# A graph layer with windows and gathers: the second lane's sort moved behind 32 unrolled sets, and sums stored by SyncE

## The chip, the cores and the metric

The kernel runs on one core of a Trainium2 chip. A time is the device time of one execution in microseconds (us). Before the change the median of 12 runs is 15380.89 us (15371.66 to 15400.01). The trace was taken from one further execution, which took 15393.0 us, with a span of 15391.4 us from its first to its last instruction.

The engines are named as in the profile: PE does the matrix products, PEld loads their weights, DVE is the vector engine, ACT the scalar engine, POOL is GpSimd, and SP is SyncE, which only issues transfers. A transfer issued by SP, ACT or POOL is moved by the core's 16 DMA engines.

## The reference

There are 100,000 nodes with 64 features, and 3,300,000 edges (1.6 million pairs in both directions and one self-loop per node), sorted by their target `dst`; `src` is random.

```
h = max(layernorm(x), 0)
x_e = concat(h[dst], h[src] - h[dst])          # one row per edge
y_e = x_e @ W.T + b
out = x + segment_sum(y_e, dst) / max(segment_count(dst), 1)
```

As the product is linear, the sums over a node's edges of `h[src]` and their count are enough. Nearly all of the work is therefore a sum of 3.3 million rows of 64 numbers, picked at random out of 100,000. The kernel keeps each row of `h` as three bf16 parts and a one (`h3`, 193 used numbers, 388 bytes), so that sums on PE are exact enough.

## The kernel before, in words

**First stage** (0 to about 450 us): `h`, `h3`, the node's own product `hb`, and zeros in the sum array `acc` (65 numbers per node, in HBM).

The edges are then handled in two ways at once.

**Windows.** The first 256 x 7968 edges are cut into 256 windows of 7968 edges each, whose targets span at most 256 nodes. Four windows make a set, so there are 64 sets in two lanes of 32 sets. For each lane `sort_lane` (L418) sorts 128 windows at once by source, each in a partition of `keys`, in a bitonic network: `exchange` (L454) copies one half of a piece to a buffer `tmp` on ACT (L455) and takes the minimum and maximum on DVE (L456, L457). The buffer is in PSUM, pieces have up to 1536 numbers. `fill_lane` (L621) then fetches the sorted keys column by column with indirect transfers of POOL (`kf` L636, `kx` L721) and stores index lists `sr_d`, `dt_d`, `et_d`, `xs_d` in HBM.

`quads` (L740) handles sets. A set goes through the 157 column tiles of `h3` (640 rows each; `tables` is a copy in HBM, three tiles to one load `tab`, L761, of 727.5 KB). In a step of two tiles DVE makes one-hot matrices `gh` (L789) and `dh` (by the helper at L340), PE picks rows with them (`pick`, `gp` L811, 12 products), ACT copies them to bf16 (`gs` L813), and PE adds them to the windows' nodes (`put`, `total` L819, 32 products). A set has 79 steps. At its end the four sums are copied (`whole` L835, which marks the end of a set in the trace), corrected on DVE, and added to `acc` by four accumulating transfers that POOL issues (L849).

**Gathers.** The other edges are 352 chunks of 28 x 128 edges (`chunks`, L345). POOL fetches 128 rows of `h3` in one indirect transfer (`nb`, L391: 9,856 of them), DVE makes a one-hot matrix `hot` of 14 x 128 columns (L340) and PE sums into `ps` (L396). The chunk's sum is added to `acc` by POOL again (L366 with indices, L371 in the loop).

**The order** is the program's order on each engine, and generators interleave it: whoever emits a piece of sort or of a set also asks for a number of gathers. The sorts of lane 0 and lane 1 follow each other (with lane 0's `fill_lane` beside lane 1's sort), paced at 1250 ns of estimated sort work per gather. Then come four sets written out, and then a hardware loop of three passes (L909) with 20 sets and 98 chunks each, about 1.7 gathers per step. Additions are put off by 56 gathers and kept 8 gathers (`GAP`) apart. At its end each pass drains its gathers and additions.

**Last stage**: a flag `odd` tells whether some assumption on the data failed (then loops repeat everything in a slow way; they run no pass otherwise); the division, the product with `W` and the sum with `x` follow in 28 steps of `acc`, `hb` and `x`.

Of the kernel before, what the change touches and what calls it, by code (L numbers as in the profile page):

```python
# [32 lines left out]
LANES = 2  # L33
SB = 20
KB = 98
U0 = 4
KG = 16
# [3 lines left out]
STEP = 1050  # L41
GAP = 8
# [19 lines left out]
PIECE = 1536  # L62
COUNTS = 1
GAIN = 2.0 ** 40
PART = 1024
TG = 3
SL = 8
SUB = 8
# [16 lines left out]
def plan(v, e):  # L85

    wl = 1 << int(np.log2(33 * CH * 1.05))
    ew = wl - PAD
    nw = LANES * P
    chunks = -(-(e - nw * ew) // CHUNK)  # L90
    return wl, nw, max(chunks, (nw // W - U0) // SB * KB)


@with_exitstack
def gnn_preln(ctx: ExitStack, tc, x, src_w, dst_w, src_p, dst_p, src_a, dst_a, wT, b, out, V, E):
# [27 lines left out]
    SETS = NL * G  # L123
    NCB = -(-V // CS)
    NE = NCB + 1
    NG = -(-NCB // SL)
    AHEAD = 8
# [3 lines left out]
    PA = NCH - (SETS - U0) // SB * KB  # L131
# [4 lines left out]
    assert 2 * C == P and NCB % 2 == 1 and PA >= 0 and SL % 2 == 0  # L136
# [9 lines left out]
    wb_d = dram.tile([SETS * W, 1], I32, name="wb_d")  # L146
    ksort = dram.tile([NL * P * WL + NT * P, 1], I32, name="ksort")
    sr_d = dram.tile([SETS, NCB, 2, P], I16, name="sr_d")
    dt_d = dram.tile([NG, P, SETS, SL * 2 * D], I16, name="dt_d")
# [25 lines left out]
    wb_r = consts.tile([1, SETS * W], I32, name="wb_r")  # L175
    turns = consts.tile([1, 2], I32, name="turns")
    ones = consts.tile([P, 1], F32, name="ones")
# [4 lines left out]
    odd = consts.tile([P, 1 + 5 * LANES], F32, name="odd")  # L182
# [22 lines left out]
    with tc.tile_pool(name="pre", bufs=2) as pre, tc.tile_pool(name="small", bufs=4) as small, \  # L205
# [32 lines left out]
        most = small.tile([P, NMT], F32, name="most", bufs=1)  # L238
        nc.vector.memset(least, 0.0)
        nc.vector.memset(most, 0.0)  # L240

        def bounds(m):
# [3 lines left out]
            nc.vector.tensor_reduce(least[:n, m:m + 1], d[:n], axis=AX.X, op=ALU.min)  # L246
            if m == NMT - 1:

                nc.vector.scalar_tensor_tensor(d[:n], d[:n], float(V), d[:n], op0=ALU.is_lt, op1=ALU.mult)
            nc.vector.tensor_reduce(most[:n, m:m + 1], d[:n], axis=AX.X, op=ALU.max)  # L250
            if m < NMT - 1:
                return
            span = small.tile([P, NMT], F32, name="span", bufs=1)
            nc.vector.tensor_sub(span, most, least)
            nc.vector.tensor_reduce(odd[:, 0:1], span, axis=AX.X, op=ALU.max)
            nc.vector.tensor_scalar(odd[:, 0:1], odd[:, 0:1], float(P), None, op0=ALU.is_ge)
# [55 lines left out]
    with tc.tile_pool(name="rows", bufs=6) as rows, \  # L312
# [5 lines left out]
        def number(at, engine, most):  # L318
            with tc.issue_after(last[engine].ins):
                return nc.values_load(at, engines=[engine], min_val=0, max_val=most)  # L320
# [4 lines left out]

        later = []
        count = [0, 0]
# [4 lines left out]
        def add_now(all_of_them=False):  # L332
            while later and (all_of_them or (later[0][0] <= count[0] and count[0] - count[1] >= GAP)):
                later.pop(0)[1]()
                count[1] = count[0]

# [8 lines left out]
        def chunks(first, n, dynamic=None):  # L345


            def load(q):
# [3 lines left out]
                nc.sync.dma_start(si[:, :k], src_p[at].rearrange("k p j -> p k j"))  # L352
                di = index.tile([P, KG, J], I32, name="di")
                nc.sync.dma_start(di[:, :k], dst_p[at].rearrange("k p j -> p k j"))
                rel = index.tile([P, KG, J], F32, name="rel", bufs=1)
                nc.vector.tensor_sub(rel[:, :k], di[:, :k], base_b[:, at][:, :, None].to_broadcast([P, k, J]))
                near = index.tile([P, KG, J, D], I16, name="near")
                nc.vector.tensor_scalar(near[:, :k], rel[:, :k, :, None].to_broadcast([P, k, J, D]), float(2 * CH), None,
                                        op0=ALU.min)
                to = index.tile([P, KG], I32, name="to", bufs=3)  # L360
                nc.vector.tensor_scalar(to[:, :k], base_b[:, at], pcol, None, op0=ALU.add)
                return si, near, to

            def addition(q, rows_to, sums):
                if dynamic is None:
                    nc.gpsimd.indirect_dma_start(  # L366
                        out=acc, out_offset=bass.IndirectOffsetOnAxis(ap=rows_to, axis=0),
                        in_=sums, in_offset=None, compute_op=ALU.add)
                else:
                    at = number(base_r[0:1, ds(dynamic + q, 1)], POOL, V)  # L370
                    nc.gpsimd.dma_start(acc[ds(at, P)], sums, accum_op=ALU.add)  # L371
# [687 lines left out]
```

## Time and profile before

| what | us |
|---|---|
| median of the runs | 15380.89 |
| profiled execution, whole / span | 15393.0 / 15391.4 |
| first gather issued by POOL | 439 |
| lane 0's sort ends (its `at_i` is made) | 1578 |
| lane 1's sort ends | 2582 |
| set 1, 4, 5 end (first `whole` copy) | 3031, 3556, 3880 |
| the loop's passes, mean distance of ends of sets | 187.3, 187.4, 186.6 |
| distance across the border of two passes | 249, 246 |
| last set ends; last stage's first load issued | 15029; 15075 |

The distances are read from the starts of the first `whole` copy of each set. A set outside the borders takes 187 us, so sixty sets make up three quarters of the time. In a row of a group view, "x2468 | 2356.2, 955 | 752.0" is the number of instructions, their busy time in us, the mean of one in ns, and the idle time of their engine just before them, with what ended it. In a row of a timeline the first two numbers are start and duration in us. "issue" is idle time for which the profile shows no cause outside the engine.

### The profile page before, as it was taken

Reading aid. Unit: us, or ns where it says so; the run is one execution under the profiler, and the core shown is the slowest. Engines: PE = TensorE matmul, PEld = TensorE weight load, DVE = VectorE, ACT = ScalarE, POOL = GpSimd, SP = SyncE. Lnnn points to the kernel's source line nnn. Section 1 sums busy time; section 2 is a strip of 40 time slices with the busy share of each in tenths; the row PEclk is TensorE's granted clock in tenths of the full one; section 3 lists DMA queues with packets and bytes.
Section 4 is the critical chain, followed back from the end, with each engine's and each line's share of the span. In section 5 each row is a group of like instructions: output and inputs, shape, how many; then the busy total and the mean of one; then the engine's idle time right before and its main releaser. Section 6 shows DMA issues by size and latency. Waiting matters only on the chain. (4 is left out here: it accounts for less than half of the span.)

```text
span 15391.4 us, 559362 instructions
## 1 busy us (share of the span) xinstructions
PE 11557.9 (75%) x238778; PEld 9470.2 (62%) x238778; DVE 11308.9 (73%) x15452; ACT 6113.0 (40%) x11710; POOL 11139.4 (72%) x11210
## 2 busy tenths in 40 slices
PE   6101001596999988998799898999879999999985
PEld 5100001475777777777677777777767777777775
DVE  6889797675777777777677777777767777777774
ACT  5335344242444444444344444444434444444441
POOL 4776766546777777777677777777777777777776
PEclk7555555798999999999899999999999999999997
DMA  7683233796999999999899999999989999999997
GB/s 294 124 104 55 48 52 76 184 310 217 317 315 310 312 305 307 307 314 302 263 315 323 306 309 305 310 307 311 304 264 311 320 312 313 307 310 310 311 303 282
DMA packets 1746424, 4097.89 MB, mean 266 GB/s; under 512 B 943899, under 2 KB 952230, under 8 KB 1738950
## 3 DMA queue, kind: packets, MB, share of 16 engines
q1 hardware_dynamic: 1182534, 3461.26, 64.5%
q0 software_dynamic: 454208, 535.92, 17.2%
q10 hardware_dynamic: 107168, 64.74, 2.4%
q8 instruction: 1877, 30.75, 0.8%
q14 instruction: 637, 5.22, 0.1%
HBM read 3880.72 MB, written 219.04 MB: 266 GB/s over the span
## 5 line engine op out<-in xcount | busy, mean ns | idle before, releaser
L391 POOL DMA_INDIRECT nb<-h,si x9856 | 9433.3, 957 | 3285.8 <-issue 2804.8
L813 ACT CAST gs<-gp 128x386 bf16<-128x386 f32 x10048 | 4837.4, 482 | 7098.5 <-PE gp L811 6869.9
L811 PE MATMUL gp<-tab,gh 128*128 128x193 bf16 x60288 | 6235.6, 251 | 942.2 <-DMA tab<-tables 562.2
L811 PEld LDWEIGHTS <-gh 128*128 128x128 bf16 x60288 | 4890.0, 99 | 1964.2 <-issue 927.9
L340 DVE TENSOR_TENSOR dh<-dt,c 128x1024 bf16<-128x1024 int16 x5056 | 3450.2, 682 | 2864.9 <-PE total L819 2719.9
L789 DVE TENSOR_TENSOR gh<-srs,c 128x1536 bf16<-128x1536 int16 x5056 | 4761.0, 942 | 18.4 <-PE gp L811 17.1
L819 PE MATMUL total<-gs,dh 32*128 32x193 bf16 x160768 | 4418.6, 247 | 37.3 <-issue 35.0
L819 PEld LDWEIGHTS <-dh 32*128 32x128 bf16 x160768 | 3198.8, 94 | 1075.7 <-issue 1056.6
L396 PE MATMUL ps<-nb,hot 128*128 128x193 bf16 x9856 | 1807.0, 263 | 2505.5 <-DVE sums L409 1870.5
L396 PEld LDWEIGHTS <-hot 128*128 128x128 bf16 x9856 | 971.3, 103 | 2466.8 <-DVE sums L409 1921.5
L455 ACT COPY tmp<-keys 128x1536 f32<-128x1536 f32 (+14 forms) x540 | 650.4, 1214 | 1238.1 <-DVE keys L457 1016.9
L456 DVE TENSOR_TENSOR keys<-tmp,keys 128x1536 f32<-128x1536 f32 (+14 forms) x540 | 755.2, 1419 | 90.4 <-ACT tmp L455 89.5
L340 DVE TENSOR_TENSOR hot<-near,c 128x1792 bf16<-128x1792 int16 x704 | 759.6, 1079 | 9.3 <-PE ps L396 9.2
L457 DVE TENSOR_TENSOR keys<-tmp,keys 128x1536 f32<-128x1536 f32 (+14 forms) x540 | 755.1, 1417 | 2.3
L849 POOL DMA_DIRECT2D acc<-wsums x256 | 348.3, 1360 | 199.6 <-DVE dh L340 60.8
L636 POOL DMA_INDIRECT kf<-ksort,at_i x322 | 310.7, 965 | 98.7 <-issue 90.4
L371 POOL DMA_DIRECT2D acc<-sums x294 | 301.8, 1027 | 15.1 <-DMA acc<-wsums 7.6
L407 DVE TENSOR_REDUCE sums<-ps 128x64 f32<-128x192 f32 x352 | 123.2, 350 | 157.0 <-PE ps L396 156.8
L839 DVE SCALAR_TENSOR_TENSOR whole<-own,whole 128x193 f32<-128x193 bf16 x512 | 190.9, 413 | 41.8 <-ACT whole L835 41.2
L303 PEld LDWEIGHTS o_ps<-w_own,hT 128*128 128x128 f32 x784 | 156.0, 253 | 81.0 <-ACT hT L298 71.1
L366 POOL DMA_INDIRECT acc<-sums,to x58 | 94.6, 1632 | 149.8 <-DVE sums L409 129.7
L721 POOL DMA_INDIRECT kx<-ksort,xat x128 | 120.8, 944 | 111.2 <-DVE xat L718 57.7
(174 smaller groups left out, 3565.4 us busy)
## 6 DMA issues: line engine op xcount, KB each, us to landing
tab<-tables SPq DMA_DIRECT2D x3328, 727.5 KB
srs<-sr_d SPq DMA_DIRECT2D x1216, 512.0 KB
nb<-h,si POOLq DMA_INDIRECT x9856
tables<-h ACTq DMA_DIRECT2D x157, 242.5 KB
h<-parts SPq DMA_DIRECT2D x28, 1358.0 KB
acc<-zeros SPq DMA_DIRECT2D x28, 910.0 KB
at<-acc SPq DMA_DIRECT2D x28, 910.0 KB
xt<-in_x SPq DMA_DIRECT2D x28, 896.0 KB
```

Of the source, the lines that this page charges most:

```text
L340: nc.vector.tensor_tensor(out.rearrange("p k (a d) -> p k a d", d=D), numbers[:, :, None].to_broadcast(shape), upto[:shape[0], :n].rearran ...
L391: last[POOL] = nc.gpsimd.indirect_dma_start(out=nb[:, j], out_offset=None, in_=h3, in_offset=bass.IndirectOffsetOnAxis(ap=si[:, u, at:at + ...
L396: nc.tensor.matmul(ps, lhsT=before[0][:, j], rhs=before[1][:, j, :CE], start=before[2] == 0 and j == 0, stop=before[2] == parts - 1 and j ...
L455: last[ACT] = nc.scalar.copy(tmp, lo)
L456: nc.vector.tensor_tensor(lo, tmp, hi, ALU.min)
L457: last[DVE] = nc.vector.tensor_tensor(hi, tmp, hi, ALU.max)
L636: last[POOL] = nc.gpsimd.indirect_dma_start(out=kf[:, c], out_offset=None, in_=ksort, in_offset=bass.IndirectOffsetOnAxis(ap=at_i[:, c0 + ...
L789: nc.vector.tensor_tensor(gh[:, :m].rearrange("p c i b s -> p (c i) b s"), srs[u, s // SL][:, c:c + m].rearrange("p c i s -> p (c i) s")[: ...
L811: nc.tensor.matmul(gp[:, i], lhsT=ghots[t][:, i, b], rhs=row[:, b + i * (NB - NR), :CE], start=b == 0, stop=b == NR - 1)
L813: nc.scalar.copy(gs[t], gp)
L819: nc.tensor.matmul(total[:, i, to(b)], lhsT=hot[at, b * P:b * P + P], rhs=of[at], start=flags.get("start", False) and b == 0, stop=flags.g ...
L849: nc.gpsimd.dma_start(acc[ds(at, CH)].rearrange("(b p) c -> p b c", p=P), sums, accum_op=ALU.add)
```

## The change

- Lane 1 is no longer sorted ahead of the sets. Lane 0 is sorted (its pieces of the first pass are 512 wide), 32 calls of its `fill_lane` follow, and then 32 sets start. In the first 69 steps (`late=True`) each step also takes four calls of `fill_lane(0)` and 4800 ns worth of POOL's fetches. From then on each step gives 0.9 units to lane 1's sort and fill (a call costs one unit and its estimated ns / 1500). Its pieces have up to 1024 numbers and its `tmp` lies in SBUF (pool `tmp`, one buffer), as PSUM is taken by the sets. In it the copy of an exchange is two calls ahead of its minimum and maximum, and all counting is left to ACT.
- The second 32 sets are written out too, without a loop. Eleven of the 53 table loads of a set are kept in SBUF for them (`kept`).
- Gathers are spread evenly: about as many per step over all sets (`pace`), chosen anew for the second half.
- `sync`, `fetched_rows` and `numbers_in` chain the instructions of SP and POOL in the order in which the program emits them.
- Sums of sets and chunks are no longer accumulated by POOL. SP stores them plainly (`put`), and reads the one row that the next one shares and writes it to `side_w` or `side_c` (`shared`), 4 gathers later (`GAP = 4`). The first three chunks' sums are kept and added at the end, where five indirect additions also put the side rows back. New flags check that ranges follow each other.
- A gather takes 128 edges in a row, so that its targets lie in a band of 32 nodes, and `hot` is written only there (`BAND`), in buffers zeroed once.
- `dt` is loaded for 32 tiles at once instead of 8, index loads are for 8 chunks instead of 16, and `rows` has 5 buffers instead of 6.

```diff
-LANES = 2
-SB = 20
-KB = 98
-U0 = 4
-KG = 16
+PARTS = (32, 32)
+U1 = 32
+KG = 8
-GAP = 8
+BEHIND = 0.9
+BAND = 32
+GAP = 4
+EARLY = 3
+KEEP = 5
-PIECE = 1536
+PIECE = (1536, 1024)
@@ chunks
-            def addition(q, rows_to, sums):
-                    nc.gpsimd.indirect_dma_start(
-                        out=acc, out_offset=bass.IndirectOffsetOnAxis(ap=rows_to, axis=0),
-                        in_=sums, in_offset=None, compute_op=ALU.add)
...
+                def put():
+                    at = number(base_r[0:1, c], SP, V)
+                    sync(acc[ds(at, P)], sums)
+
+                def shared():
+                    at = number(base_r[0:1, after], SP, V)
+                    sync(side_c[c], acc[ds(at, 1)])
+
+                add_later((LAG - 1) * J, put)
+                add_later((LAG - 1) * J + GAP, shared)
@@ sort_lane
+            def both(part, n):
+                finish = part()
+                if soft:
+                    yield 0
+                    yield 0
+                finish()
+                yield 2.083 * n + 290
@@ quads, the same for the four sums of a set
-                        nc.gpsimd.dma_start(acc[ds(at, CH)].rearrange("(b p) c -> p b c", p=P), sums, accum_op=ALU.add)
+                    sync(acc[ds(at, CH)].rearrange("(b p) c -> p b c", p=P), sums)
...
+                if s < NCB and s % TG == 0 and kept is not None and s // TG % KEEP == 0:
+                    tabs[u, s // TG] = kept[:, s // TG // KEEP]
@@ the order
+                    begin = fill_lane(0, fill, took)
+                    for _ in range(4 * SL):
+                        next(begin)
+                    rest = behind_quads()
+                    left = 0.0
+                    pace = (NCH * J - count[0]) / ((SETS - 1) * NE // 2)
+                    for i, _ in enumerate(quads(0, U1, late=True)):
+                        if i < NE // 2 - 10:
+                            for _ in range(4):
+                                next(begin, None)
+                            gathers(FILL)
+                        else:
+                            drain(begin)
+                            left += BEHIND
+                            with behind_hots():
+                                while left > 0:
+                                    left -= 1 + next(rest, 0) / 1500
+                            gathers(pace * GATHER)
                     drain(rest)
+                    add_now(True)
...
+                pace = (NCH * J - count[0]) / ((SETS - U1) * NE // 2 - 4)
+                for _ in quads(U1, SETS - U1, kept):
+                    gathers(pace * GATHER)
                 drain(ev)
                 add_now(True)
-                with tc.For_i(0, (SETS - U0) // SB, 1) as g:
...
+                for q, sums in enumerate(early):
+                    at = number(base_r[0:1, q:q + 1], POOL, V)
+                    nc.gpsimd.dma_start(acc[ds(at, P)], sums, accum_op=ALU.add)
```

## The prediction

> **What bounds the kernel now.** I read the page's slices first, then stages, then POOL's groups inside the loop, then PE's waits there.
>
> ```profile
> core 0: us, PE busy (x) PEld busy (x) DVE busy (x) ACT busy (x) POOL busy (x), PEclk, DMA share, GB/s
> 500.00:1590.00 1090.00, 115.40 (x756) 101.06 (x756) 993.99 (x955) 427.82 (x466) 774.22 (x777) 0.54 0.56 80
> 1590.00:2590.00 1000.00, 74.73 (x423) 57.14 (x424) 845.36 (x1123) 397.01 (x449) 691.45 (x714) 0.52 0.29 50
> 3217.00:3566.00 349.00, 323.38 (x7112) 264.67 (x7110) 263.42 (x369) 150.02 (x313) 169.31 (x171) 0.98 0.93 308
> ```
>
> The stages: lane 0's sort, lane 1's sort, and two of the written-out sets. The sorts keep DVE busy (994 of 1090 us) and leave PE at a tenth; the sets keep PE busy and DVE at three quarters. In the sets with few gathers POOL is half idle.
>
> ```profile
> L391 POOL DMA_INDIRECT nb<-h,si x2468 | 2356.2, 955 | 752.0 <-issue 701.1 <-DMA nb<-h,si 21.3 <-PE gp L811 18.0
> L849 POOL DMA_DIRECT2D acc<-wsums x72 | 98.2, 1364 | 57.2 <-DVE dh L340 22.7 <-DVE gh L789 15.8 <-DMA acc<-wsums 9.1
> L371 POOL DMA_DIRECT2D acc<-sums x89 | 91.6, 1029 | 0.1
> L778 POOL DMA_INDIRECT rows_x<-h,xs x36 | 34.8, 967 | 11.0 <-issue 11.0
> ```
>
> These are POOL's groups from 4000 to 7400 us, in the loop's first pass. Busy and idle together are 3108 + 155 + 92 + 46 = 3401 us, the whole window, and the idle part is a constant 0.30 us after every gather:
>
> ```profile
> 5013.41 0.94 POOL L391 DMA_INDIRECT nb<-h,si  x1 [0.30 <-issue]
> 5014.66 0.95 POOL L391 DMA_INDIRECT nb<-h,si  x1 [0.30 <-issue]
> ```
>
> One gather per 1.25 us is all that POOL does, so POOL bounds the loop, although the page gives it 72%. A gather costs (2356.2 + 752.0) / 2468 = 1.259 us there. Per set: 137 gathers and 2 of `rows_x` make 175 us, four `acc<-wsums` at 2.16 us 8.6, 4.9 `acc<-sums` at 1.03 us 5: 189 against 187 measured. PE is close behind:
>
> ```profile
> PE gp L811 <- DMA tab<-tables: 142.7, 174, 3.1
> PE ps L396 <- DMA nb<-h,si: 76.6, 73, 4.2
> ```
>
> PE's undisturbed step takes 2.07 us with two gather products in it and 2.00 with one (timeline at 5000 us). So a set is 79 x 1.92 + 0.08 per gather + 6 at its end, 169 us with 137 gathers, and 8 us of waiting for tables (142.7 / 18 sets) make 177. The written-out sets with 80 gathers or so took 171 to 178 us.
>
> **The change part by part.** The sum goes along the time axis of this profile.
>
> *To the end of lane 0's sort.* It ends at 1578 us. The 51 `hot` in it shrink from 1.08 us (1792 numbers) to 0.39 (448 numbers; read from `dh` forms of 1024 in 0.686 and 512 in 0.421), 35 us less on a DVE that is the bound; 512-wide first pieces add 5. First-stage `bounds` gets eight more passes over 3584 numbers, about 30 us of DVE where it has a third of its time free: 0 to 15; I take 0. End: 1548.
>
> *First set.* Lane 0's fill now lies in front. 32 fetches at 1.25 us are 40, and 10 for the store and reload of the lists. Then 69 steps at 4800 ns of fetches, which POOL needs in full: 331 us. Ten ordinary steps 23, and 20 for the end that waits for the last lists. 424 us: set 1 ends at 1972.
>
> *How many gathers remain.* Lane 0's yields sum to 876 us, so 701 gathers are asked for. The first set asks for 265 fetches, 225 of them the fill's (161 `kf`, 64 `kx`), so 40 gathers. 9115 remain. The pace is (9856 - 701) / 4977 = 1.84 fetches per step; the first half's other 2459 steps ask for 4523, including lane 1's 225. That is 145.4 per set. 4817 are left for 32 sets, 150.5 each.
>
> *POOL without sums.* 294 + 256 + 58 accumulations leave POOL (302 + 348 + 95 us busy). Per set in the first half 147.4 fetches x 1.259 = 185.6 us, in the second 152.5 x 1.259 = 192.0.
>
> *Lane 1 behind 31 sets.* Its calls cost 2043 units, 2270 of the 2459 steps at 0.9: it just fits, with no burst at the end. DVE's load per set, from the loop's rows: `gh` 74.9 us, `dh` 54.3, `eh`, `whole` and sums 10.6, narrow `hot` 10.4 x 0.39 = 4, together 144. Lane 1 adds 755 us of minima and maxima (half of the page's two rows), 15 for 69 more pieces, 64 before and 155 after the sort, so 989 / 31 = 32. 176 of 192 us, 92%. ACT: 78 us per set, and 18 more for copies (325 us and more per lane) and counts. PE: 1.92 x 79 + 0.08 x 145 + 6 + 8 = 178. All lie under POOL; I take no stall from them, and keep their failure as a rival.
>
> *Two SBUF inputs.* Before, `tmp` was in PSUM. Now minimum and maximum of lane 1 read two SBUF operands. The trace has DVE instructions of that form beside gathers at the start of the sort:
>
> ```profile
> 475.93 1.28 DVE L447 COPY_PREDICATED s<-own,q 128x1024 int32<-128x1024 int32 x1
> 476.19 1.86 POOL L391 DMA_INDIRECT nb<-h,si  x1 [0.30 <-issue]
> ...
> 477.85 1.22 DVE L443 TENSOR_TENSOR own<-s,keys 128x1024 int32<-128x1024 int32 x1
> 478.36 1.53 POOL L391 DMA_INDIRECT nb<-h,si  x1 [0.30 <-issue]
> ...
> 698.37 1.73 DVE L457 TENSOR_TENSOR keys<-tmp,keys 128x1530 f32<-128x1530 f32 x1
> 699.13 0.94 POOL L391 DMA_INDIRECT nb<-h,si  x1 [0.30 <-issue]
> ```
>
> The gather that starts inside such an instruction takes 1.5 to 1.9 us; the one beside an exchange with `tmp` in PSUM takes 0.94. From 450 to 520 us 48 gathers take 1158 ns each, 10 us more than at 944, beside 20 such instructions: 0.5 us each. A pair of 2.4 us delays one gather, perhaps a second: between 0 and 1.0 us; I take 0.6. 339 pairs make 203 us on the engine that bounds, between 0 and 339.
>
> The Trainium skill (SBUF — State Buffer, Who interferes with whom) says that a DVE instruction with two SBUF inputs contends with a GpSimd instruction that reads SBUF, and that the second to start blocks fully until the first is done. This speaks against the change; if gathers were held for the whole of both instructions, 339 x 2.4 = 820 us would be lost and the sum would be 15,118, while by the rows above it is 203.
>
> *SP.* It gets two transfers for each of 256 + 349 sums, in order with its table loads, and each waits for the landing of the one before. In the loop a 1 KB load of SP (`xs`) lands 4.9 us after its issue in the median, 6.8 at most (DMA records of 58 of them), and the pairs are 4 gathers, 5.0 us, apart: between 0 and 1.8 us of standing, I take 0.3. 18 per set, 5 us, which delay table loads that wait for a free buffer anyway. PE has 14 us per set of cover under POOL. Cost nothing; the cover ends at 0.8 us each.
>
> *Transfers.* `kept` takes a fifth of the table bytes off the second half, `dt` has a quarter of its packets: at best the 8 us of waits per set, hidden under POOL. `KG`, five `rows` buffers: nothing, POOL still leads by 70 gathers. Unrolling: the instruction queues already moved 36 MB for 559,362 instructions, so the loop saved no fetch; its borders (249 and 246 us instead of 187, and the drain before it) go, one switch of pools comes: 25 us.
>
> *Tail.* Before, 362 us from the last set's `whole` to the end. The five last additions (one each 3.75 us) leave POOL, 24 less; six pairs on SP at 6 us follow, 36; three early additions 11, five side additions with their indices 20: 405.
>
> **Sum**: 1548 + 424 + 31 x (185.6 + 6.5) + 25 + 32 x 192.0 + 405 = 14,501 us. The profiled execution (15391.4) stands 0.07% above the median of the runs; on that scale 14,490.
>
> **Rivals.**
> 1. *Gathers are not held up.* The pairs run on DVE where gathers slip between: the 203 us and part of the 25 go, and POOL's bare 1.25 us holds: 14,501 - 203 - 60 = 14,240. For it: the fetch reads only an index column. Against: 1.86 and 1.53 above.
> 2. *DVE's queue becomes the bound of the first half.* DVE at 92% with a pair of 2.4 us where a step leaves 0.44 us free; `gh` has three buffers. At 205 us per set it is 13 x 31 = 400 more: 14,900. For it: the DVE waits for PE's release in the loop (788.6 us in 18 sets) are all its slack, 44 us per set, and lane 1 uses 32. Against: those waits show it ahead of PE.
> 3. *SP starves the tables; slower than before.* Stores and reads stand in SP's queue in front of `tab`. From 178 us PE must reach 192 + 880 / 63 = 206 per set, 1.6 us for each of 18 pairs' halves. Fully exposed at 3.75 us it would be 245, and 17,800. For it: SP stands 1,575 us before `tab` in 18 sets, so it never is ahead by more than three buffers. Against: 5.0 us of spacing.
> 4. *The slow way is taken* because a new flag rises: many times the time. From the reference's inputs the windows' first nodes are at least 235 apart and chunks reach 7 of the band's 16, so this is nearly out.
>
> **How the numbers follow.** My case 0.45 (14,330 to 14,700), rival 1 0.18, rival 2 0.24, rival 3 0.12 (most of it above 15,400), rival 4 0.01. Faster by over 0.2%, about what a measurement can tell, is all but rivals 3 and 4, and small milder forms: 0.87; within 0.2% 0.01; slower 0.12. The range takes in rival 1 without its full 60 us and rival 2 with a little more: 14,170 to 15,000, leaving out rivals 3 and 4 and some 0.07 at the ends.
>
> **What would show it.** POOL's four rows should become two, with a gather to gather distance of 1.25 us in both halves and more than 0.95 us of duration beside lane 1's pairs. Sets should end 192 us apart in both halves. `ACT tmp` and `DVE keys` should run up to about the 30th set. PE's wait for `tab` should stay near 8 us per set. Wrong would be: PE waiting for `gh` by tens of us per set (rival 2), or for `tab` with SP standing before `acc<-wsums` (rival 3).

## The result, and the profile after

The changed kernel takes 15,144.9 us in the median of 7 runs (15,128.9 to 15,197.1) beside 15,383.3 us for the kernel before, a ratio of 0.9847 with a 95% interval of 0.9838 to 0.9856. It is faster, as forecast, but by 238 us and not by 890, and it lies above the predicted range. The profiled execution has a span of 15,152.9 us.

The stages of the changed kernel, in the same columns as before: the sets 2 to 24, which have lane 1's sort beside them; the sets 25 to 30, which have lane 1's fill beside them; and the sets of the second half.

```profile
core 0: us, PE busy (x) PEld busy (x) DVE busy (x) ACT busy (x) POOL busy (x), PEclk, DMA share, GB/s
1989.90:6793.00 4803.10, 4045.81 (x84367) 3317.01 (x84366) 3772.88 (x5369) 2147.79 (x4240) 3374.44 (x3401) 0.94 0.87 281
6793.00:8250.00 1457.00, 1076.37 (x21844) 879.59 (x21842) 898.72 (x1579) 540.26 (x1114) 859.75 (x906) 0.87 0.91 251
8650.00:14780.00 6130.00, 5516.01 (x117912) 4539.55 (x117909) 4222.15 (x6430) 2466.97 (x5153) 4596.02 (x4864) 0.96 0.84 264
```

The second half is what was forecast: 6130 us for 32 sets, 191.6 each with the switch of pools. PE is busy 90% of it. In the sets 2 to 24 PE is busy 84% and DVE 79%, in the fill PE 74%: there neither is full, and the time must be in waits. The distances between the `whole` copies give the account, against the sum of the prediction (14,501 in the time of the profile):

| Step | Predicted, us | Measured, us | Difference |
|---|---|---|---|
| end of lane 0's sort | 1548 | 1460 | -88 |
| first set | 424 | 529 | +105 |
| sets 2 to 24, each | 192.1 | 209.3 | +396 in all |
| sets 25 to 30, each | 192.1 | 242.7 | +304 in all |
| sets 31 and 32, together | 384 | 390 | +6 |
| switch and second half | 6169 | 6131 | -38 |
| tail | 405 | 373 | -32 |

The differences sum to 653 us; the spans differ by 652. So the miss lies in the first half. POOL's groups there, from 2500 to 6400 us (mean duration of one; idle time before, and what ended it):

```profile
L353 POOL DMA_INDIRECT nb<-h,si x2729 | 2717.0, 996 | 833.7 <-issue 800.1 <-DMA nb<-h,si 15.5 <-PE gp L917 14.0
L353 POOL DMA_INDIRECT rows_x<-h,xs x36 | 34.4, 956 | 315.1 <-DMA xs<-xs_d 294.9 <-issue 20.2
```

A gather costs (2717.0 + 833.7) / 2729 = 1.301 us. The prediction had 1.259 and 6.5 us a set for the held ones (gathers that last longer beside lane 1's DVE instructions), 1.303 in all. That price was right, and yet POOL is not the bound: for 295 us it stands in front of `rows_x`, waiting for the last lists of a set, 16 us in each of the 18.6 sets of the window. POOL is ahead of the quads and waits for them. PE's waits in the same window (who waited for whom: total us, number, longest us):

```profile
PE ps L450 <- DVE sums L464: 263.5, 89, 8.3
PE gp L917 <- DVE gh L891: 218.7, 165, 7.4
PE gp L917 <- DMA tab<-tables: 98.3, 108, 5.0
```

The two longest of DVE's waits in the same window, in the same columns:

```profile
DVE gh L891 <- DMA srs<-sr_d: 563.9, 207, 8.3
DVE gh L891 <- PE gp L917: 201.0, 153, 5.5
```

The waits of SP's queue there, three of which are for transfers that it issued itself:

```profile
SPq L349 <- PE gp L917: 2136.8, 805, 10.8
SPq L349 <- DMA side_w<-acc: 136.3, 48, 5.7
...
SPq L349 <- DMA acc<-wsums: 61.2, 32, 4.5
SPq L349 <- DMA acc<-sums: 54.0, 31, 4.0
```

PE waits 580 us, 31 us a set; 8 were forecast, all for tables. Most of it is for DVE: for its sums of the gathered rows (there is one PSUM buffer `ps`) and for its one-hots `gh`. But DVE isn't full. It stands 564 us, 30 us a set, before `gh`, because the index list `srs` has not landed. In the whole run of the kernel before this wait is 1.3 us:

```profile
DVE gh L789 <- DMA srs<-sr_d: 1.3, 1, 1.3
```

The reason stands in SP's queue of the kernel before, from 4000 to 7400 us, in a line that the prediction did not use:

```profile
SPq L752 <- DVE gh L789: 430.1, 257, 6.7
```

L752 is the load of `srs`. Before, SP stood at this load until `gh` had released a buffer, and issued it that moment: in the median 19.6 us before the first `gh` that uses it (from the issue and the DVE record of each group of eight tiles). In the changed kernel the queue runs in program order and the load is issued where `fetch(t + AHEAD)` stands in the text, eight tiles ahead: 7.0 us in the median of the sets 2 to 24 (6.8 in the second half), whatever buffers are free.

What such a wait does to PE is seen in the timeline of the changed kernel:

```profile
4004.19 0.51 PE L925 MATMUL total<-gs,dh 32*128 32x193 bf16 x16
...
4007.53 0.35 DVE L462 TENSOR_REDUCE sums<-ps 128x64 f32<-128x192 f32 x1
...
4007.99 0.34 PE L450 MATMUL ps<-nb,hot 128*128 128x193 bf16 x1 [3.29 <-DVE sums L464]
...
4009.03 2.12 PE L917 MATMUL gp<-tab,gh 128*128 128x193 bf16 x12
...
4010.79 0.31 PEld L450 LDWEIGHTS <-hot 128*128 128x128 bf16 x2
```

PE stood 3.29 us for the sums, and the next 12 products took 2.12 us; undisturbed ones take 1.19. The granted clock tells why. This is the stretch in which it was lowered:

```profile
core 0: us, PE busy (x) PEld busy (x) DVE busy (x) ACT busy (x) POOL busy (x), PEclk, DMA share, GB/s
4007.44:4014.27 6.83, 6.28 (x73) 4.88 (x74) 4.74 (x8) 1.17 (x3) 5.23 (x5) 0.50 0.50 170
```

The clock went to half at 4007.44 us, 2.7 us after PE's last product before the stall had ended, and stayed there for 6.83 us. The Trainium skill (TensorE: Matmul & The Clock Gate, "What's actually happening") says that the PE's clock falls to half after an idle window of about 3.4 us; the half agrees with this stretch, the idle time before it was shorter here. The granted clock of the whole stage is 0.94, beside 0.96 in the second half.

### The profile page after: what moved, and what is told of

It reads as the page before. It is cut to its first block, busy times and chain, and to the rows that moved or that the text cites. A ratio compares the mean times of both kernels' runs of the same rounds, so it can differ in the third digit from the quotient of the medians.

```text
span 15152.9 us, 552351 instructions
## 1 busy us (share of the span) xinstructions
PE 11787.1 (78%) x238778; PEld 9700.1 (64%) x238778; DVE 10761.7 (71%) x15750; ACT 6130.6 (40%) x11927; POOL 10460.2 (69%) x10611
## 5 line engine op out<-in xcount | busy, mean ns | idle before, releaser
L353 POOL DMA_INDIRECT nb<-h,si x9856 | 9487.8, 963 | 3086.2 <-issue 2864.7
L917 PE MATMUL gp<-tab,gh 128*128 128x193 bf16 x53952 | 5717.0, 256 | 1208.3 <-DVE gh L891 615.8
L917 PEld LDWEIGHTS <-gh 128*128 128x128 bf16 x60288 | 5052.1, 101 | 2232.5 <-issue 1048.9
L925 PE MATMUL total<-gs,dh 32*128 32x193 bf16 x160768 | 4531.0, 251 | 34.4 <-issue 28.2
L925 PEld LDWEIGHTS <-dh 32*128 32x128 bf16 x165888 | 3338.1, 95 | 1148.1 <-issue 1117.5
L519 ACT COPY tmp<-keys 128x1024 f32<-128x1024 f32 (+15 forms) x609 | 674.6, 1115 | 618.0 <-DVE keys L525 461.7
L524 DVE TENSOR_TENSOR keys<-tmp,keys 128x1024 f32<-128x1024 f32 (+15 forms) x609 | 773.6, 1280 | 76.7 <-ACT tmp L519 75.2
L525 DVE TENSOR_TENSOR keys<-tmp,keys 128x1024 f32<-128x1024 f32 (+15 forms) x609 | 775.0, 1282 | 11.6
L917 PE MATMUL gp<-kept,gh 128*128 128x193 bf16 x6336 | 677.1, 252 | 45.9 <-DVE gh L891 45.6
L353 POOL DMA_INDIRECT rows_x<-h,xs x128 | 121.7, 951 | 755.5 <-DMA xs<-xs_d 711.8
L353 POOL DMA_INDIRECT kf<-ksort,at_i x322 | 307.9, 956 | 317.1 <-ACT k L768 140.2
L384 DVE TENSOR_TENSOR hot<-near,c 128x448 bf16<-128x448 int16 x704 | 267.0, 379 | 0.0
L320 PE MATMUL o_ps<-w_own,hT 128*128 128x128 f32 x784 | 197.9, 389 | 15.5 <-ACT hT L315 14.9
L353 POOL DMA_INDIRECT kx<-ksort,xat x128 | 121.1, 946 | 108.6 <-DVE xat L810 69.9
## 6 DMA issues: line engine op xcount, KB each, us to landing
tab<-tables SPq DMA_DIRECT2D x2976, 727.5 KB
```

The costliest lines, as they stand in the source:

```text
L320: nc.tensor.matmul(o2[:, i], lhsT=hT[:, i], rhs=w_own.rearrange("p a c -> p (a c)"), start=False, stop=True)
L353: last[POOL] = nc.gpsimd.indirect_dma_start(out_offset=None, **how)
L384: nc.vector.tensor_tensor(out.rearrange("p k (a d) -> p k a d", d=D), numbers[:, :, None].to_broadcast(shape), upto[:shape[0], :n].rearran ...
L519: ins = nc.scalar.copy(tmp, lo)
L524: nc.vector.tensor_tensor(lo, tmp, hi, ALU.min)
L525: ends_at(nc.vector.tensor_tensor(hi, tmp, hi, ALU.max))
```

## The experiments

The kernels of the experiments hold the changed kernel with 14 more lines ahead of the helpers, so that L353 there is L367 and so on. "Sets" are the mean distances of the `whole` copies in us. Five kernels leave work out or read the wrong lists, so that their sums are not the layer's (no_lane1, no_sums_stored, no_list_stores, no_lane1_lists_early_2, three_edits); these ran once each, both_sorted_first ten times and the other experiments of this table four times. Executions of one kernel of the table lay at most 68 us apart. The changed kernel comes first; three runs that were far slower follow in the text:

| Run | Time, us | First set ends | Sets 2-24 | Sets 25-30 | Second half |
|---|---|---|---|---|---|
| the changed kernel | 15,145 | 1989 | 209.3 | 242.7 | 191.2 |
| no_lane1 | 14,423 | 1948 | 199.7 | 201.1 | 184.1 |
| no_sums_stored | 14,894 | 1968 | 203.5 | 237.5 | 190.9 |
| no_list_stores | 14,931 | 1956 | 209.4 | 211.7 | 191.0 |
| both_sorted_first | 15,349 | 2736 | 207.6 | 195.6 | 182.9 |
| lists_early_2 | 14,848 | 1956 | 200.3 | 235.2 | 191.0 |
| both_first_lists_early_2 | 15,065 | 2732 | 199.6 | 190.5 | 181.0 |
| no_lane1_lists_early_2 | 14,177 | 1944 | 194.5 | 193.3 | 182.2 |
| lists_early_gap | 14,766 | 1959 | 196.8 | 231.8 | 191.1 |
| three_edits | 14,572 | 1955 | 197.2 | 201.8 | 191.1 |
| all_kept | 14,926 | 2731 | 187.8 | 180.2 | 181.2 |
| all_kept_paced | 14,423 | 2729 | 185.1 | 178.0 | 176.0 |

### The parts of the change taken out one by one

**no_lane1** leaves out lane 1's sort and fill; the second half reads lane 0's lists.

```diff
-                    rest = behind_quads()
+                    rest = iter(())
...
+            lists = base % U1
...
-                        sr_d[ds(base + u, 1), s:s + m]...
+                        sr_d[ds(lists + u, 1), s:s + m]...
```

> The changed kernel without any work of lane 1: no second sort and no second fill; the second 32 sets read lane 0's lists and windows again (so their sums are wrong), and the flag is held at zero. SP's stores and read-backs of sums stay. Theory A (the work of lane 1 behind the sets holds PE up, through DVE's queue in the sort and through the list stores in the fill): sets 2 to 30 end 185 to 190 us apart instead of 209 and 243, the first half is 600 to 750 us shorter, and PE's wait for DVE's sums falls from 14 us per set to under 5. Theory B (SP, standing before its stores and read-backs, hands out index lists and tables late): the distance stays at 200 us or more, with DVE still waiting about 30 us per set for srs.

Measured: 14,423 us; the sets 2 to 24 at 199.7, the sets 25 to 30 at 201.1. Lane 1's sort costs 9.6 us a set and no more, its fill 41.6. The first half is 511 us shorter; the rest of the 722 us lies in the second half, which has fewer gathers left. Theory A's forecasts all missed (185 to 190 us a set, a first half 600 to 750 us shorter, and under 5 us a set of waiting for sums, where 9.7 were measured); theory B's 200 us is nearer. DVE's wait for the lists is still there, and larger, as DVE comes to it earlier (the waits of no_lane1 from 2500 to 6400 us):

```profile
DVE gh L906 <- DMA srs<-sr_d: 1010.3, 290, 9.3
```

This speaks against the prediction's rival 2: with a fifth less to do in a set (0.65 of 199.7 us instead of 0.79 of 209.3), DVE waits longer for the lists and PE still waits 189.5 us for sums and 167.6 us for `gh`. The same window gives the price of a held gather. POOL's gathers in no_lane1, and then one of the two instructions of lane 1's pairs in the changed kernel:

```profile
L367 POOL DMA_INDIRECT nb<-h,si x2840 | 2682.8, 945 | 866.0 <-issue 825.7 <-PE gp L932 19.5 <-DMA nb<-h,si 18.0
```

```profile
L525 DVE TENSOR_TENSOR keys<-tmp,keys 128x1024 f32<-128x1024 f32 (+11 forms) x293 | 339.6, 1159 | 7.1
```

Without lane 1's pairs 2840 gathers take 945 ns each, with 293 pairs 2729 take 996. That is (2717.0 - 2729 x 0.945) / 293 = 0.47 us for a pair; 0.6 was taken.

**no_sums_stored** leaves out the stores of all sums that SP has taken over, and the reads behind them.

```diff
-                    else:
-                        keep(before[3], sums)
...
-                    keep(u, i, sums)
```

> The changed kernel without the stores and read-backs of sums on SP and without the side additions at the end (the sums are computed and not stored). Lane 1's sort and fill stay. Theory A: sets 2 to 24 still end 203 us or more apart, sets 25 to 30 240 or more. Theory B: sets 2 to 24 end 195 us or less apart, and DVE's wait for srs falls from 30 us per set to under 10. The second half stays at 191 us per set by both, as POOL bounds it.

Measured: 14,894 us, 251 less, at 5.8 us a set for the sets 2 to 24 and about as much in the fill. 43 of the 251 are in the tail, which the prediction priced by itself; the step "Cost nothing" is wrong by the rest, some 208. Theory A held for the sets 2 to 24 (203 or more) and missed for the fill (240 or more); theory B missed, as the sets stay over 195 us and DVE still waits 25 us a set for the lists. PE's wait for `tab` falls from 98.3 to 51.4 us and DVE's for `srs` from 563.9 to 483.7: both kinds of load stand behind the stores.

**no_list_stores** leaves out only the stores of lane 1's finished lists (sort, fetches and arithmetic of the fill remain); the second half reads lane 0's lists, as in no_lane1.

```diff
-                    sync(*waiting.pop(0))
+                    to, of = waiting.pop(0)
+                    if l == 0:
+                        sync(to, of)
...
```

> The changed kernel with lane 1's sort and fill, but the fill's lists of lane 1 are not stored; the second half reads lane 0's lists (so its sums are wrong), and the flag is held at zero. Theory C (the fill's 512 KB and 32 KB stores in small packets, in SP's queue and on the 16 DMA engines, collide with the table loads): sets 25 to 30 end 205 to 215 us apart instead of 243. Rival (the fill's work on DVE, ACT and POOL, or SP's order, is the cost): they stay at 230 or more. The sets before the fill stay at 209 by both.

Measured: 14,931 us, 214 less. The sets 2 to 24 stay as they are (209.4), the sets of the fill fall from 242.7 to 211.7: 31 us in each of six, 186 us, as theory C has it. The trace's count of packets for the stretch from 7050 to 7900 us, of the changed kernel:

```profile
DMA packets 172553, 200.60 MB, mean 236 GB/s; under 512 B 132309, under 2 KB 134485, under 8 KB 172429
```

And of no_list_stores, in the same stretch:

```profile
DMA packets 78636, 228.53 MB, mean 269 GB/s; under 512 B 30604, under 2 KB 33164, under 8 KB 78488
```

The list stores bring 100,000 small packets into 850 us, fewer bytes move in all, and yet the 16 DMA engines are busy 92% of the stretch instead of 83%. PE's wait for `tab` there, in the changed kernel and in no_list_stores:

```profile
PE gp L917 <- DMA tab<-tables: 125.2, 25, 10.1
```

```profile
PE gp L934 <- DMA tab<-tables: 15.5, 16, 3.4
```

The stores stand in SP's queue ahead of the tables too; how much of the loss is their packets and how much their place in the queue was not taken apart. The Trainium skill (DMA: Bandwidth & Descriptors, "Why small descriptors are slow") says that each packet and each descriptor has a fixed cost, so that small ones lose bandwidth; 236 GB/s at 92% beside 269 GB/s at 83% agree in their sign.

**both_sorted_first** undoes the move: both lanes are sorted ahead of all quads, with lane 0's fill beside lane 1's sort, and only lane 1's fill lies thinly beside the sets; everything else of the change stays.

```diff
-BEHIND = 0.9
+BEHIND = 0.2
...
-            soft = l > 0
+            soft = False
...
-                    for i, ns in enumerate(sort_lane(0, keys(), piece, few, ps)):
+                    for l in range(NL):
+                        rest = fill_lane(l - 1, fill, took) if l else iter(())
+                        for i, ns in enumerate(sort_lane(l, big.tile([P, WL], F32, name="keys"), piece, few, ps)):
```

> The changed kernel with one part undone: both lanes are sorted before the first set, as before the change (two key buffers, tmp in PSUM, lane 0's fill beside lane 1's sort), and only lane 1's fill lies behind the sets, thinly (0.2 units per step). All else of the change stays. Theory A: the sets end 180 to 187 us apart, the second sort costs 1000 us in front, and the whole takes 14,300 to 14,800 us, faster than both kernels. Theory B: the sets stay at 200 us or more and the whole takes 15,500 us or more.

Measured: 15,348.8 us, a ratio of 0.9987 (0.9978 to 0.9997) to the kernel before. With no sort beside them the sets 2 to 24 still take 207.6 us. Theory A failed; of theory B the sets held (200 or more), the total (15,500 or more) did not. The waits told more (DVE in both_sorted_first, 2500 to 6400 us):

```profile
DVE gh L905 <- DMA srs<-sr_d: 1014.6, 256, 17.7
```

So what slows the first half is neither lane 1's sort on DVE nor the stores alone. This led to theory D: SP's program order hands out the index lists too late.

### The lists asked for earlier

**lists_early** makes one edit: the load of `srs` is issued eight tiles earlier.

```diff
-            def fetch(t):
+            def rows_to_pick(t):
                 u, s = divmod(t, NE)
-                if u >= n:
-                    return
-                if s < NCB and s % SL == 0:
+                if u < n and s < NCB and s % SL == 0:
                     m = min(SL, NCB - s)
                     srs[u, s // SL] = sr = load.tile([P, SL, 2, P], I16, name="srs")
...
+            def fetch(t):
+                if late and t < NE + SL:
+                    rows_to_pick(t)
+                if not late or t >= NE:
+                    rows_to_pick(t + SL)
+                u, s = divmod(t, NE)
...
```

> One edit to the changed kernel: the load of an index list (srs, on SyncE, eight tiles at a time) is issued eight tiles earlier than before, so that two groups of eight are under way instead of one; the first set keeps its old places. Nothing else moves. Theory D (the list is handed out late because SyncE's queue now runs in program order; VectorE's one-hot waits for it, loses its lead over TensorE, the sums of the other half arrive late, and TensorE waits and loses clock): VectorE's wait for srs goes from 207 ns an instruction to under 60, the first half's sets 2 to 24 from 209.3 to 190 to 196 us, the fill's sets 25 to 30 from 242.7 to 225 to 235, the whole to about 14,700 us. Rival E (VectorE's queue is simply full of lane 1's sort, and the wait for the list is time it would lose elsewhere): sets 2 to 24 stay at 203 us or more and the whole within 100 us of 15,145.

This run answers nothing: in its round the kernel before took 24,524 us, and this one 25,796 (ratio 1.0518). The two kernels that went with it, both_first_lists_early and no_lane1_lists_early, took 25,916 and 25,241. All three were run again under names that end in _2; the last section returns to this round.

> The same kernel as lists_early. On the chip of that run the kernel before itself took 24,524 us instead of 15,383, and TensorE waited 5.5 ms for its own instructions ahead of the total products alone, so the run says nothing on the question; this one is to answer it on a chip where the kernel before takes about 15,380 us. Theory D (late lists): VectorE's wait for srs under 60 ns an instruction, sets 2 to 24 from 209.3 to 190 to 196 us, the fill's sets from 242.7 to 225 to 235, the whole about 14,700 us. Rival E (VectorE's queue is full, the wait only shows time it would lose elsewhere): sets 2 to 24 at 203 us or more, the whole within 100 us of 15,145.

Measured: 14,847.7 us, ratio 0.9651 (0.9635 to 0.9667), 297 us less than the changed kernel. DVE's wait for `srs` is gone from the list of waits between 2500 and 6400 us, and PE's wait for the sums is halved (PE's waits of lists_early_2 there):

```profile
PE gp L938 <- DMA tab<-tables: 237.0, 173, 6.1
PE ps L464 <- DVE sums L478: 135.3, 72, 6.0
PE gp L938 <- DVE gh L912: 70.4, 36, 4.6
```

The load now comes 14.4 us ahead of its first use in the median of the sets 2 to 24. Rival E (sets at 203 or more, total within 100 us) falls; D's mechanism holds, but its size was half right: sets of 200.3 where it gave 190 to 196. The wait for tables rose from 98 to 237 us, and DVE waits for `dt`, which the change loads 32 tiles at a time and which no run asked for earlier (DVE's waits of lists_early_2, same window):

```profile
DVE dh L398 <- DMA dt<-dt_d: 176.7, 69, 5.6
```

A wait was taken away, and the next in line took a part of the gain.

The second half limits what a late list can be blamed for. In the changed kernel its lists come as late as in the first, and DVE waits for them there too (9000 to 14000 us, 26 us a set):

```profile
DVE gh L891 <- DMA srs<-sr_d: 682.7, 271, 8.4
```

Yet lists_early_2 leaves the sets of that half at 191.0 us, beside 191.2: there POOL fills the time, and the late list costs next to nothing.

> The same kernel as both_first_lists_early, for the same reason. Theory D: sets of the first half from 207.6 to 180 to 187 us, the whole 14,500 to 14,700 us. Rival E: no change, sets at 200 us or more, the whole above 15,200.

Measured: 15,065.5 us, ratio 0.9799 (0.9783 to 0.9816): 283 us less than both_sorted_first, but sets of 199.6. Neither D (180 to 187) nor E (200 or more, and above 15,200) held.

> The same kernel as no_lane1_lists_early (lane 1's sort and fill left out, lane 0's lists read in both halves, so the output is not the reference's), for the same reason. Theory D: sets of the first half from 200 to 184 to 190 us, the whole about 14,100. If the tables loaded anew are the limit instead, they stay at 195 or more.

Measured: 14,176.6 us, sets of 194.5 where D gave 184 to 190, and 195 or more was to mean the tables. The wait for tables is 286.9 us here. In all three, 5 to 9 us a set came from the lists, and a first half without any sort is still 12 to 19 us a set slower than the second.

### The order of the stores, and whether the losses add up

**lists_early_gap** is lists_early with one number changed, so that SP's stores of sums and the reads behind them come at least six gathers apart.

```diff
-GAP = 4
+GAP = 6
```

> lists_early (14,848 us) with GAP 6 instead of 4: the delayed stores of sums, and the reads of their first row that follow each store, are handed to SyncE at least six gathers apart instead of four. Theory F (in the first half SyncE stands some 0.06 of the time on its own earlier stores, side_w<-acc 140 us, acc<-wsums 72 and acc<-sums 52 of 3,900 us, and the tables behind them come late): these waits fall to under 130 us together, TensorE's wait for tab from 237 to under 170 us, the sets 2 to 24 from 200.3 to 195 to 198, the whole to about 14,760. Rival G (the tables are late because only three buffers hold them, or because the transfers are full, and SyncE's waits lie in time it would wait for a buffer anyway): the waits fall, the sets stay at 199 or more and the whole within 50 us of 14,848.

Measured: 14,765.7 us, ratio 0.9597 (0.9581 to 0.9614); sets 2 to 24 at 196.8. SP's waits for its own transfers in the window, 307 us in lists_early_2 (147.3, 86.0 and 74.1), are 45 us now (33.0, 6.5 and 5.2; three rows of SP's queue of lists_early_gap, 2500 to 6400 us):

```profile
SPq L363 <- DMA acc<-wsums: 33.0, 15, 4.0
SPq L363 <- DVE dh L398: 29.2, 60, 2.8
SPq L363 <- DMA side_w<-acc: 6.5, 5, 2.3
```

So the stores did hold up what stood behind them (theory F is right in time and sets, and rival G, with 199 us or more, falls); PE's wait for `tab` fell only to 201.7 us, where under 170 was expected, so that tables remain late for another reason too. And POOL has become the bound, with the price that the prediction gave it (POOL's groups of lists_early_gap in that window):

```profile
L367 POOL DMA_INDIRECT nb<-h,si x2897 | 2880.8, 994 | 883.0 <-issue 839.4 <-DMA nb<-h,si 20.1 <-PE gp L938 19.5
L367 POOL DMA_INDIRECT rows_x<-h,xs x40 | 40.0, 1000 | 96.7 <-DMA xs<-xs_d 80.1 <-issue 16.6
```

Busy and idle are 3,900 of 3,900 us, and only 80 of them, 4 us a set, are a wait for lists.

**three_edits** is lists_early_gap without the stores of lane 1's lists, as in no_list_stores.

> lists_early_gap with the stores of lane 1's finished lists left out (lane 0's lists are read in both halves, so the output is not the reference's). If the losses of the changed kernel are the late lists (297 us), the list stores (214) and the order of the sum stores, and they add up, the whole is 14,500 to 14,600 us, the fill's sets 200 to 205; if they overlap, it is above 14,680.

Measured: 14,572 us, the fill's sets at 201.8. The losses add up: 297 for the lists, 82 for the order of the stores and 194 for the list stores are 573 of the 655 us between the forecast and the result, each measured on top of those before it.

### The tables kept through all sets

**all_kept** is both_first_lists_early with a single run of 64 sets, in which one table in six (for room, instead of one in five) stays in SBUF.

```diff
-KEEP = 5
+KEEP = 6
-                    for i, _ in enumerate(quads(0, U1)):
-                        left += BEHIND
+                    for i, _ in enumerate(quads(0, SETS, kept)):
+                        if i < (U1 - 1) * NE // 2:
+                            left += BEHIND
...
```

> both_first_lists_early with one run of 64 sets in place of two of 32, so that one table in six (one in five before, in the second half alone) stays in SBUF through all sets; the fill of lane 1 lies beside the first 31. If the tables loaded anew are what keeps the first half of both_first_lists_early at 199.6 us a set where its gathers need 165, its sets come to 176 to 186 us, and with 2,742 us up to the first set's end and 373 of a tail the whole to 14,330 to 14,800. If it is the fill of lane 1 beside it (its gathers, list stores and VectorE work), the first 31 sets stay at 192 or more and the whole at 14,750 or above.

Measured: 14,926.2 us, ratio 0.9704 (0.9688 to 0.9720). The sets 2 to 24 fall from 199.6 to 187.8, 1.8 us above the range that was to mean tables and below the 192 that was to mean the fill. PE's wait for `tab` from 2800 to 6400 us, in both_first_lists_early_2 and in all_kept:

```profile
PE gp L938 <- DMA tab<-tables: 374.8, 169, 11.7
```

```profile
PE gp L938 <- DMA tab<-tables: 209.6, 72, 11.4
```

So the tables loaded anew are most of the 19 us by which this first half was slower than the second; 6.6 us a set remain to the second half, with the fill beside the sets. The total missed for another reason: 628 us follow the last set, since the pace did not count the 225 fetches that the fill makes in place of gathers.

**all_kept_paced** counts them, and takes GAP 6.

```diff
-GAP = 4
+GAP = 6
-                    pace = (NCH * J - count[0]) / (SETS * NE // 2)
+                    pace = (NCH * J - count[0] + NCB + NO // 2 + SPILL) / (SETS * NE // 2)
```

> all_kept (14,926 us) with two numbers changed: the 225 fetches of lane 1's fill are counted in the pace of the gathers (in all_kept they took the place of gathers, so that 628 us followed the last set's end instead of 373), and GAP 6 instead of 4. If all_kept's tail is that miscount, 628 falls to about 375, each set takes 3.5 more gathers (0 to 4 us on sets of 181 to 188 us), and the stores' order gives 0 to 3 us a set in the first half: the whole is 14,580 to 14,760 us. If the tail is something else, it stays above 550 and the whole above 14,850.

Measured: 14,422.9 us, ratio 0.9388 (0.9372 to 0.9403), the fastest kernel that does the whole work, and 722 us below the changed kernel. The tail is 386 us, so the miscount explains it; the total is 157 us better than the forecast's lower end, because the sets became shorter (176.0 in the second half), not longer by the gathers that they took on. In its second half both engines are nearly full. The two halves of all_kept_paced (columns as in the stages above), and POOL's groups from 8600 to 13970 us:

```profile
2741.00:8400.00 5659.00, 5179.67 (x113405) 4298.44 (x113403) 4211.42 (x6493) 2425.30 (x5021) 4128.21 (x4365) 0.97 0.91 282
8600.00:13970.00 5370.00, 5075.26 (x112025) 4212.61 (x112023) 4050.84 (x6052) 2347.47 (x4911) 4057.98 (x4296) 0.99 0.90 292
```

```profile
L367 POOL DMA_INDIRECT nb<-h,si x4234 | 4000.3, 945 | 1290.6 <-issue 1226.8 <-PE gp L938 31.1 <-DMA nb<-h,si 28.4
L367 POOL DMA_INDIRECT rows_x<-h,xs x62 | 58.5, 944 | 21.8 <-issue 18.3 <-DMA xs<-xs_d 3.5
```

PE is busy 95% of the second half at a granted clock of 0.99. POOL's rows add up to the whole of it, with 3.5 us of waiting for lists; sets are shorter than the changed kernel's because more gathers were made earlier, 139 a set here instead of 150 (4234 in 5370 / 176.0 = 30.5 sets).

Which of its two edits shortened the sets was not taken apart.

## Why the prediction was right or wrong

- *The end of lane 0's sort: "It ends at 1578 us"*, and 30 us less after the change. The end was read right, its content wrong: while lane 0's positions are counted, the kernel before already runs lane 1's exchanges between the counts. From 450 us to the end of the stretch it has 299 pairs of exchanges, the changed kernel 270. The 29 that went with lane 1 are 89 us of DVE (422.8 + 421.6 - 378.2 - 377.6), and the sort ended 88 us earlier than forecast. The narrow `hot` was right: 0.377 us for 0.39.
- *First set, 424 us.* 529. The sum counted POOL's fetches alone. In the profile ACT waits 125.0 us before `t` for `dt_d<-t` to land and PE waits 184.3 us for `gh`, with all DMA engines busy (a share of 1.01 from 1460 to 1725 us). The list stores of lane 0 are the likely cause by what lane 1's cost; no run took them out.
- *POOL without sums, 1.259 us, and the held gathers, 6.5 us a set.* Right: 1.301 us a gather measured, 1.303 predicted; 0.47 us a pair for 0.6. That the sum agrees so closely is partly luck: a gather without pairs took (2682.8 + 866.0) / 2840 = 1.250 us in no_lane1, so the pairs added 0.051 instead of 0.044, as more of them fell on each gather. Rival 1 (no gather held, 14,240) is refuted, and so is a lock for the whole of both instructions, 2.3 us a pair ((338.8 + 339.6) / 293).
- *"All lie under POOL; I take no stall from them."* This failed. The single sums of DVE (176 of 192 us) and PE (178, 8 of them a wait) were near enough: in the sets 2 to 24 DVE is busy 164 us a set and PE 176. But a sum of busy times says nothing about when the inputs arrive.
- *"SP ... Cost nothing; the cover ends at 0.8 us each."* This is the step that failed. It priced only the stores, and only by how they delay tables. Program order also moved the list loads, which the scheduler had issued 19.6 us ahead of use and which now come 7.0 us ahead. With the lists early and the stores wider apart, 379 us of the miss are gone. The step's own cover was thin as well: leaving the stores out gives 251 us, 43 of them in the tail.
- *"Transfers ... hidden under POOL."* This failed too. It counted what the change takes off and not what it moves, and put the list stores at nothing. Before, lane 0's were issued beside lane 1's sort, which needs no tables, and lane 1's beside the first set (2590 to 2855 us). Now lane 0's lie beside the first set, and lane 1's (from 6800 to 7850 us) beside the sets 25 to 30, which load tables of 727.5 KB. Lane 1's cost 194 to 214 us, 186 of them in these six sets.
- *Second half 192.0 a set, tail 405.* 191.6 with the switch, and 373.
- *Rival 2 (14,900)* is nearest in time and named the place, PE waiting for `gh`, but not the cause: DVE waited itself for 30 us a set. *Rival 3*'s queue was the right one, with the wrong load behind it and a size of 6 us a set instead of 68. Rival 4 did not happen.

What stays open: the 82 us between three_edits and the forecast, and why the tables stay late after the stores are spread. In three_edits the sets 2 to 30 are still 176 us over the forecast, and all else is under it (69 us are left in the time of the profile): the first set ends 18 us earlier than forecast, the sets 31 and 32 take 14 us less, the second half 42 and the tail 33.

## What to carry to other kernels

When a queue is taken from the scheduler and put into program order, list every transfer in it with its lead before (issue to first use), and give each at least that lead in the new order; the lead of the costliest transfer is not that of the others. An engine's price per operation can be right and still not set the time: before calling an engine the bound, look in its rows of the stage for idle time that another engine or a transfer ends, as POOL's 16 us a set here. When work is moved beside other work, its stores move too: here 100,000 small packets came with them, and the DMA engines moved fewer bytes in more of the time.

## What the runs showed of the hardware that was not expected

A chain of dependent transfers on one queue cost the queue more than its instructions here. Each store of sums is followed by a read of a row that it wrote, SP waits for each to land, and in the changed kernel it stood 251 us of 3900 for that (136.3, 61.2 and 54.0). With the lists early it stood 307, and two more gathers between them left 45. The Trainium skill (DMA: Bandwidth & Descriptors, "Two DMAs through the same engine are not ordered") says that a dependent transfer has to wait for the completion of the first at the engine that issues it; these rows show what is queued behind that wait.

Gathers were held by 0.47 us for a pair of DVE instructions with two SBUF inputs, while DVE's own instructions did not get longer: its exchanges of 1024 numbers take 1.22 us with `tmp` in SBUF (lane 1) and 1.22 with `tmp` in PSUM (lane 0).

In one round of runs everything took 1.6 to 1.8 times the usual time. There PE stood still between its own instructions, with no engine or transfer named as the cause. The group of the `total` products of lists_early, the run of that round:

```profile
L946 PE MATMUL total<-gs,dh 32*128 32x193 bf16 x160768 | 6409.3, 264 | 5520.9 <-issue 5499.5
```

PE's wait ahead of the same products in lists_early_2, the same kernel in the next round:

```profile
PE total L946 <- issue: 28.6, 36, 2.7
```

The first line is of the whole run, 5.5 ms of idle time; the second is of 3900 us in the later run, 28.6 us. A gather took 953 ns in the slow round (963 in the changed kernel), and both instruction queues moved the same 35 MB; the mean granted clock was 0.717 instead of 0.895. The three kernels, with different work, came within 3% of each other. That would fit a limit in how fast instructions reach PE, but no run shows it. The cause stays open, also whether it was the chip: the record names chip 4 for this round and for two later ones, in which the kernel before took 15,375 and 15,372 us.
